# A convolution as four products side by side in the array, tokens added in place, and eight-bit tokens ahead of the FFN's transposes

## The chip, the cores and the metric

The kernel runs on one core of a Trainium2 chip. The metric is device time in microseconds of that core; lower is better. The batch of 32 images is processed in one launch.

## What is computed

The input is x, 32 images of 56 x 56 positions with 96 channels, in float32. Two layers follow each other (the weights' folding is left out here):

```python
# layer 0
h  = layernorm(x) @ w_in + b_in           # only the first 192 of 384 outputs are used
x  = x + silu(conv3x3(h, conv_w) + conv_b)  # 192 -> 96 channels, SAME padding
# layer 1, on t = x as 3136 tokens of 96 channels
a  = relu(bn1(layernorm(t) @ w1.T))       # 192 channels
X  = fft(a, axis=tokens)
X  = relu(X.re*rd - X.im*id + rb) + 1j * relu(X.im*rd + X.re*id + ib)
t  = t + bn2(ifft(X).real @ w2.T)
y  = relu(qlinear(layernorm(t), W1, b1))  # operands rounded to 8-bit floats (5, 2), sums to 16-bit
t  = t + qlinear(y, W2, b2)
```

## The kernel before

**Tiling.** An image's 3136 tokens lie as 112 partitions of 28 tokens (token = 28p + j). Partition p is half of an image row, and j is the place in that half. Work goes by groups of 4 values of j (seven groups g) or by chunks of 8, 8, 8 and 4 values (`LN_CHUNKS`).

**The convolution.** The layernorm's scaled tokens `xa` (L372) are multiplied by a constant matrix (`image`, L153), which both transposes them to channels and forms, for every four output rows, six sums of input rows; ScalarE copies them into the buffer `img` (L154). A convolution along rows then needs six products (k) of three column shifts (dx) each, instead of 4 x 3 taps x 3 shifts. `conv` (L164) does them for one chunk of j: a unit has three parts, each with two values of k and three shifts, so six matmuls of 97 rows and 96 columns of weights over 2 x n x 14 columns (224 for a chunk of 8, 112 for the chunk of 4). Part 0 is copied by ScalarE (`m`, L167), parts 1 and 2 are combined by VectorE (`sd`, L175, L176, L188, and the four output rows `s`, L183), ScalarE applies silu (L191), TensorE transposes back to tokens (`st`, L196), and VectorE adds the input (`t <- st, x`, L398). For that addition the input is loaded a second time into a buffer `x`, one DMA per chunk (L349); the first load, `xl` (L364), feeds the layernorm.

**The rest of an image.** Per group: a transpose (`tp_n`, L146), the product with w1 (`ph`, L209), relu on ScalarE (L212), the first DFT stage (`pa`, L218), a store to a DRAM scratch (`da`) and loads back in another order (`at`). Then the second stage (`px`, L233; for its third kind, u = 2, the two halves of the output are 64-column products written to partitions 0 to 63 and 64 to 127), the frequency-wise relus on both engines (`av`, `sv`, `gt`), the product with w2 and the first inverse stage (`pg`, L272 and L276, `pe`, L286), a store `de`, loads `y`, and the last stage (`py`, L294), added to `t` (L474). The FFN normalizes four tokens at a time (`xn`, float32, L488), transposes them (`tp_n`, L146), rounds them to 8 bits on ScalarE while copying them out of PSUM (`n3t`, L300), and multiplies (`pf`, L305, `po`, L322). `ffn_end` adds the result to `t` into a buffer `o` (L332), from which the output is stored (L510).

**Order.** The program is written as a plan: each step of each image has a time (`put(when, ...)`), in units of which an image takes eight, and steps are issued sorted by it. A later image starts eight units after the one before, so about four images are in flight. A scheduling pass then fixes each engine's order from these priorities and the dependencies. [...] All the DMAs of the main loop are issued by SyncE.

**Buffers.** The PSUM tag "q" (two buffers) is shared by `im`, `cv` and `st`. `pf` has one buffer. `tpool` keeps `t` of three images; `xpool` holds two of the second loads.

Two places of the plan, since their numbers matter later:

```python
for part in range(3):
    put(at + ats[part], conv_part, i, part)     # at = CONV + 2 * i, ats = (0, 0.5, 1.25)
CONV, FIRST, BACK, FFN = -12.3, -8, 8.5, 10.85
```

Of the kernel before, what the change touches and what calls it, by code (L numbers as in the profile page):

```python
# [45 lines left out]
C = 96  # L46
# [15 lines left out]
LN_CHUNKS = ((0, 8), (8, 16), (16, 24), (24, 28))  # L62


LN_W, LN_B, CONV_B, B_IN, BN1, BN2, NPAR = 0, 1, 2, 3, 5, 13, 17
# [15 lines left out]
def hybrid_kernel(ctx: ExitStack, tc: tile.TileContext, x, par, spar, w_in, conv_w, w1, w2, fw1, fb1, fw2, fb2, fa, fb, ib, ia, rows6, out):  # L81
# [7 lines left out]
    make_identity(nc, ident)  # L89
    mhalf = const.tile([N1, N2], F32, name="mhalf")  # L90
# [9 lines left out]
    convb = par_sb[:, CONV_B : CONV_B + 1]  # L100
# [40 lines left out]
    def to_channels(xs, b, g, kind):  # L141

        rows = xs.shape[2]
        ps = psum.tile([rows, G4, N1], F32, tag="tp", name=f"tp_{kind}_{b}_{g}")
        for j in range(G4):
            nc.tensor.transpose(ps[:, j, :], xs[:, j, :], ident[:N1, :N1])  # L146
        return ps

    def image(xa, n, b, j0):

        ps = psq.tile([C + 1, n, 2, WC * WG], F32, tag="q", name=f"im_{b}_{j0}")
        for j in range(n):
            nc.tensor.matmul(ps[:, j], xa[:, j, :], rows6_sb, start=True, stop=True)  # L153
        nc.scalar.copy(img[:, :, j0 + 1 : j0 + 1 + n].rearrange("c h j k g -> c j h (k g)"), ps)  # L154

    def conv(s, part, b, i):

        j0, j1 = LN_CHUNKS[i]
        n = j1 - j0
        ps = s[part] = psq.tile([C, 2, 2, n, WG], F32, tag="q", name=f"cv_{b}_{i}_{part}")  # L160
        for at, k in enumerate(PAIRS[part]):
            for dx in range(3):
                cols = img[:, :, j0 + dx : j1 + dx, k, :]
                nc.tensor.matmul(ps[:, at], wv[:, k, dx, :], cols, start=(dx == 0), stop=(dx == 2))  # L164
        if part == 0:
            m = s["m"] = work.tile([C, 2, 2, n, WG], F32, tag="m", name=f"m_{b}_{i}")
            nc.scalar.copy(m, s.pop(0))  # L167

    def conv_sums(s, b, i):

        j0, j1 = LN_CHUNKS[i]
        n = j1 - j0
        m, ps = s.pop("m"), s.pop(1)
        sd = s["sd"] = work.tile([C, 2, 2, 2, n, WG], F32, tag="sd", name=f"sd_{b}_{i}")
        nc.vector.tensor_tensor(sd[:, 0], m, ps, ALU.add)  # L175
        nc.vector.tensor_tensor(sd[:, 1], m, ps, ALU.subtract)  # L176
        s["y"] = work.tile([C, n, WG, 4, 2], F32, tag="s", name=f"s_{b}_{i}")
# [3 lines left out]
    def conv_row(s, r, at, scale):  # L181
        row = s["y"][:, :, :, r, :].rearrange("c j g h -> c h j g")
        nc.vector.scalar_tensor_tensor(row, s["sd"][:, at, 1], scale, s["sd"][:, at, 0], ALU.mult, ALU.add)  # L183

    def conv_silu(s):
# [5 lines left out]
        nc.scalar.activation(s["y"], s["y"], AF.Silu, bias=convb)  # L191

    def to_tokens(s, b, g):
        pt = psq.tile([N1, G4, C], F32, tag="q", name=f"st_{b}_{g}")
        for j in range(G4):
            nc.tensor.transpose(pt[:, j, :], s[:, j].rearrange("c r i h -> c (r i h)"), ident[:C, :C])  # L196
        return pt
# [131 lines left out]
    def ffn_add(y1, tg, o, b, g):  # L329
        y2 = work.tile([N1, G4, C], F16, tag="y2", name=f"y2_{b}_{g}")  # L330
        nc.vector.tensor_tensor(y2, y1, b2q, ALU.add)
        nc.vector.tensor_tensor(o, tg, y2, ALU.add)  # L332

    class Image:


        def __init__(self, b):
# [3 lines left out]
            self.x, self.t, self.s, self.n2t, self.hq = {}, {}, {}, {}, {}  # L341
# [3 lines left out]
        def load(self, i):  # L345
            j0, j1 = LN_CHUNKS[i]
            self.t[i] = tpool.tile([N1, j1 - j0, C + 1], F32, tag=f"t{i}", name=f"t_{self.b}_{i}")
            self.x[i] = xpool.tile([N1, j1 - j0, C], F32, tag="x", name=f"x_{self.b}_{i}")
            nc.sync.dma_start(self.x[i], self.tokens[:, j0:j1, :])  # L349

        def group(self, g, tiles=None):
            return (tiles or self.t)[g // 2][:, g % 2 * G4 : (g % 2 + 1) * G4, :]
# [21 lines left out]
    def make_image(im, i, j, n):  # L374
        image(im.xa[i][:, j : j + n], n, im.b, LN_CHUNKS[i][0] + j)

# [5 lines left out]
    def conv_part(im, i, part):  # L382
        if part == 0:
            im.s[i] = {}
        conv(im.s[i], part, im.b, i)

    def conv_first(im, i):
        conv_sums(im.s[i], im.b, i)

    def conv_last(im, i):  # L390
        conv_silu(im.s[i])

    def conv_tokens(im, g):
        im.held["st", g] = to_tokens(im.s[g // 2]["y"][:, g % 2 * G4 :], im.b, g)

    def conv_end(im, g):

        nc.vector.tensor_tensor(im.group(g)[:, :, :C], im.held.pop(("st", g)), im.group(g, im.x), ALU.add)  # L398
        for i in ended(g):
            im.rs[i] = stats(im.t[i], "b", im.b, i)  # L400

    def deviation(im, i):

        _, var, rs = im.rs[i]
        nc.vector.tensor_tensor(im.t[i][:, :, C], var, rs, ALU.mult)
# [65 lines left out]
    def back_end(im, g):  # L471
# [3 lines left out]
        for i in ended(g):  # L475
            mu, _, rs = stats(im.t[i], "c", im.b, i)
            im.norm[i] = mu, None, rs

    def normal(im, g, j):

        i = g // 2
        if j == 0:
            im.xc[g] = xnp.tile([N1, G4, C], F32, tag="xn", name=f"xn_{im.b}_{g}")
        mu, _, rs = im.norm[i]
        xc = im.xc[g]
        for j in (j, j + 1):
            at = g % 2 * G4 + j
            nc.vector.tensor_scalar(xc[:, j], im.t[i][:, at, :C], mu[:, at : at + 1], rs[:, at : at + 1], ALU.subtract, ALU.mult)  # L488
# [15 lines left out]
    def ffn_end(im, g):  # L504
        o = im.held["o", g] = work.tile([N1, G4, C], F32, tag="o", name=f"o_{im.b}_{g}")
        ffn_add(im.held.pop(("y1", g)), im.group(g)[:, :, :C], o, im.b, g)

    def store(im, g):
        o = im.held.pop(("o", g))
        nc.sync.dma_start(im.result[:, g * G4 : (g + 1) * G4, :], o)  # L510
# [8 lines left out]
    def plan(b):  # L519
# [5 lines left out]
        for i, (j0, j1) in enumerate(LN_CHUNKS):  # L525
            last = i == len(LN_CHUNKS) - 1

            at = CONV - 8 + 2 * (i + 1)
            ats = (-0.95, -0.7) if last else (0.2, 0.5, 0.85) if i == 2 else (0.25, 1.0, 1.5)
            put(at + ats[0] - (2.5 if b else 12), fetch, i)  # L530
            put(at + ats[0] - 1.15, take_in, i)
            for part, j in enumerate(range(0, j1 - j0, 3)):
                put(at + ats[part], make_image, i, j, min(3, j1 - j0 - j))

            at = CONV + 2 * i
            put(at + 0.6, im_load, i)
            ats = (0, 0.35, 0.7) if last else (0, 0.5, 1.25)
            for part in range(3):
                put(at + ats[part], conv_part, i, part)
            put(at + ats[1] + 0.2, conv_first, i)  # L540
            put(at + ats[2] + 0.2, conv_last, i)
            for g, off in zip(range(j0 // G4, j1 // G4), (1.85, 2.75)):
                put(at + off, conv_tokens, g)
                put(at + off + 0.15, conv_end, g)
            put(FIRST + 2 * i - 0.75, deviation, i)
        put(CONV - 0.6, make_seam)
        for g in range(NG):
# [7 lines left out]
            put(max(BACK - 0.6, at - 2.9), fetch_y, g)  # L555
# [27 lines left out]
    def im_load(im, i):  # L583
        im.load(i)

    CONV, FIRST, BACK, FFN = -12.3, -8, 8.5, 10.85
# [14 lines left out]
    run(CONV - 0.1)  # L601

    with tc.tile_pool(name="setup", bufs=1) as sp, tc.tile_pool(
# [4 lines left out]
        nc.sync.dma_start(spar_sb, spar)  # L608
        win = sp.tile([C, H], F32, name="win")
# [242 lines left out]
```

## Time and profile before

| | us |
|---|---|
| median of 3 runs (lowest to highest) | 3248.47 (3239.42 to 3249.1) |
| the profiled execution: its time, its span | 3247.36, 3245.6 |
| TensorE matmul busy, in the span | 3167.5 (98%) |
| TensorE weight load busy | 2737.2 (84%) |
| VectorE busy | 2529.4 (78%) |
| ScalarE busy | 2196.2 (68%) |
| GpSimd busy | 598.2 (18%) |
| granted TensorE clock, mean | 0.986 of full |
| DMA engines' mean busy share | about 0.4 |

The page is of one profiled execution. Its own time stands 1.1 us below the median, and its span is 1.8 us shorter than its time. A float32 matmul of the program appears as two records, each with its own weight load; a transpose and an eight-bit matmul appear as one. Matmuls are pipelined: a record's duration is longer than the time until the next record can start, so the starts of consecutive records tell what one costs.

### The profile page before, as it was taken

The page shows a single profiled execution, that of the slowest core. Times are in us where ns is not written, and L with a number is a line of the kernel's source. Part 1 is how long each engine was busy: PE and PEld are TensorE (multiplying, and loading weights), DVE is VectorE, ACT ScalarE, POOL GpSimd, SP SyncE. Part 2 cuts the span into 40 slices and gives each one's busy share as a digit, 9 for nine tenths or more (in the row PEclk, how much of TensorE's full clock was granted, in tenths as well). Part 3 has the DMA queues.
Part 4 walks back from the last instruction along what each step waited for, and adds up shares of the span by engine and source line. Part 5 has one row for each costly group of instructions (what it writes and reads, how often), then busy time and mean ns, then how long its engine had stood idle before and what let it go on. Part 6 is the DMA issues. An engine that isn't in the chain of part 4 may idle for free.

```text
span 3245.6 us, 66513 instructions
## 1 busy us (share of the span) xinstructions
PE 3167.5 (98%) x23701; PEld 2737.2 (84%) x23701; DVE 2529.4 (78%) x7829; ACT 2196.2 (68%) x5232; POOL 598.2 (18%) x397
## 2 busy tenths in 40 slices
PE   7999999999999999999999999999999999999997
PEld 6888888888888888888888888888888888888875
DVE  5557878877877877877877887878787878787777
ACT  2556676766776676766676766667667667767676
POOL 1211212111212111212121121111121112121111
PEclk8999999999999999999999999999999999999997
DMA  4343344343344433344333344333344333443341
GB/s 109 94 116 103 93 122 122 111 115 101 104 122 117 115 109 108 106 118 120 108 103 106 109 127 122 101 109 105 109 127 117 108 109 95 120 124 97 103 118 56
DMA packets 334551, 355.43 MB, mean 110 GB/s; under 512 B 129305, under 2 KB 287401, under 8 KB 333993
## 3 DMA queue, kind: packets, MB, share of 16 engines
q1 hardware_dynamic: 332210, 349.01, 38.6%
q8 instruction: 187, 3.06, 0.4%
q10 hardware_dynamic: 2008, 2.17, 0.2%
q14 instruction: 146, 1.19, 0.1%
HBM read 196.93 MB, written 154.14 MB: 108 GB/s over the span
## 4 chain that ended last, share of the span: by engine, by line
PE 87%; DMA 7%; DVE 3%; ACT 1%; issue 1%; SPq 0%; POOL 0%; ACTq 0%; DVEq 0%; POOLq 0%
PE cv L164 21%; PE px L233 9%; PE ph L209 9%; PE pa L218 8%; PE im L153 7%; PE tp_n L146 5%; PE pg L276 5%; PE pe L286 5%; PE pg L272 5%; PE py L294 4%; PE pf L305 4%; PE po L322 4%; DMA de<-es 2%; PE st L196 2%; DMA at<-da 2%; DMA y<-de 1%
## 5 line engine op out<-in xcount | busy, mean ns | idle before, releaser
L164 PE MATMUL cv<-img,wv 97*96 97x224 f32 (+1 forms) x4608 | 874.7, 330 | 0.2
L164 PEld LDWEIGHTS cv<-img,wv 97*96 97x96 f32 x4608 | 671.3, 164 | 101.0 <-issue 16.4
L138 POOL TENSOR_TENSOR rs_c<-var_c,mhalf 112x8 f32<-112x8 f32 (+1 forms) x128 | 198.3, 1549 | 1404.5 <-DVE var_c L136 1039.0
L307 ACT CAST h<-pf 128x448 f16<-128x448 f32 x672 | 362.2, 539 | 87.2 <-PE pf L305 86.4
L138 POOL TENSOR_TENSOR rs_b<-var_b,mhalf 112x8 f32<-112x8 f32 (+1 forms) x128 | 193.9, 1515 | 1194.7 <-DVE var_a L136 592.8
L233 PEld LDWEIGHTS px<-fb_sb,at 112*64 112x64 f32 (+1 forms) x3584 | 329.7, 165 | 94.7 <-issue 42.0
L212 ACT ACTIVATE h<-ph,rs_b 112x192 f32<-112x192 f32 x896 | 330.0, 424 | 105.7 <-PE ph L209 102.6
L233 PE MATMUL px<-fb_sb,at 112*64 112x112 f32 (+3 forms) x3584 | 378.2, 273 | 21.7 <-DMA at<-da 19.3
L209 PE MATMUL ph<-w1a,n2t 97*112 97x192 f32 x1792 | 380.2, 329 | 3.3 <-DVE sv L252 2.0
L218 PE MATMUL pa<-h,fa_sb 112*112 112x384 f32 x896 | 366.7, 491 | 0.3 <-DVE t L398 0.3
L315 DVE TENSOR_SCALAR h<-h,b1q 128x448 f16<-128x448 f16 x658 | 216.4, 329 | 178.1 <-ACT h L307 170.4
L153 PE MATMUL im<-rows_sb,xa 112*97 112x168 f32 x1792 | 333.4, 312 | 11.3 <-DVE xa L372 10.1
L209 PEld LDWEIGHTS ph<-w1a,n2t 97*112 97x112 f32 x1792 | 288.9, 177 | 32.1 <-DVE sv L252 2.6
L249 DVE SCALAR_TENSOR_TENSOR sv<-px,spar_sb,av 128x224 f32<-128x224 f32 (+2 forms) x352 | 153.9, 437 | 183.3 <-ACT av L240 180.7
L153 PEld LDWEIGHTS im<-rows_sb,xa 112*97 112x97 f32 x1792 | 262.9, 167 | 25.1 <-DVE xa L372 10.1
L219 ACT COPY u<-pa 112x384 f32<-112x384 f32 x448 | 216.2, 482 | 80.7 <-PE pa L218 76.3
L316 DVE CAST hq<-h 128x448 fp8e5<-128x448 f16 x672 | 259.2, 386 | 11.7 <-ACT h L313 6.7
L305 PE MATMUL pf<-n3t,w1q 96*128 96x448 fp8e5 x672 | 243.1, 362 | 7.4 <-ACT h L307 6.2
L276 PE MATMUL pg<-w2x,gt 128*112 128x96 f32 (+1 forms) x1792 | 245.3, 260 | 0.0
L322 PEld LDWEIGHTS <-hq 128*112 128x112 fp8e5 x2688 | 198.5, 135 | 51.7 <-DVE hq L316 16.9
L276 PEld LDWEIGHTS pg<-w2x,gt 128*112 128x112 f32 (+1 forms) x1792 | 239.8, 178 | 1.0
L488 DVE TENSOR_SCALAR xn<-t,st_c,rs_c 112x96 f32<-112x96 f32 x896 | 231.7, 324 | 10.1 <-POOL rs_c L138 7.3
(115 smaller groups left out, 6121.7 us busy)
## 6 DMA issues: line engine op xcount, KB each, us to landing
da<-u SPq DMA_DIRECT2D x224, 336.0 KB, 2.9
at<-da SPq DMA_DIRECT2D x224, 336.0 KB, 4.8
de<-es SPq DMA_DIRECT2D x448, 84.0 KB, 2.5
y<-de SPq DMA_DIRECT2D x224, 168.0 KB, 3.0
out<-o SPq DMA_DIRECT2D x224, 168.0 KB, 2.6
xl<-in_x SPq DMA_DIRECT2D x96, 336.0 KB, 3.5
x<-in_x SPq DMA_DIRECT2D x96, 336.0 KB, 4.0
xl<-in_x SPq DMA_DIRECT2D x32, 168.0 KB, 2.3
```

The lines of the kernel that those rows point to most:

```text
L138: nc.gpsimd.tensor_tensor(rs, var, mhalf[:, :n], ALU.pow)
L153: nc.tensor.matmul(ps[:, j], xa[:, j, :], rows6_sb, start=True, stop=True)
L164: nc.tensor.matmul(ps[:, at], wv[:, k, dx, :], cols, start=(dx == 0), stop=(dx == 2))
L209: nc.tensor.matmul(ph[:, j, :], n2t[:, 2 * j2 + j, :], w1a, start=True, stop=True)
L212: nc.scalar.activation(h[:, j], ph[:, j], AF.Relu, scale=rs[:, 2 * j2 + j : 2 * j2 + j + 1])
L218: nc.tensor.matmul(pa, fa_sb, h, start=True, stop=True)
L233: nc.tensor.matmul(px[rows, j], lhs, fb_sb[:, first(p) : first(p + 1)], start=True, stop=True)
L276: nc.tensor.matmul(pg[:, half, j, :], lhs, w2x, start=False, stop=True, skip_group_check=True)
L305: nc.tensor.matmul(pf, w1q[:, k * 128 : (k + 1) * 128], n3t, start=True, stop=True)
L307: nc.scalar.copy(h1, pf)
L316: nc.vector.tensor_copy(hq[:, k, :], h2, saturate=False)
L322: nc.tensor.matmul(po[:, j, :], hq[:, k, j * N1 : (j + 1) * N1], w2q[:, k, :], start=(k == 0), stop=(k == 2))
```

## The change

The unit of the convolution is now a third of the output channels over all columns, in place of all channels over a chunk of columns. A unit r has 32 output channels. The 28 columns of a half row are cut into NT = 4 stretches of CT = 7, and each stretch's product goes to its own 32 partitions of the output: four matmuls with the same 32 columns of weights and different moving data. An image has three units of three parts; a part has 2 k x 3 dx x 4 stretches = 24 matmuls of 196 columns. All but the first of a part are issued at high priority and kept in program order, so that little comes between them.

The tokens of x are put in another order beforehand (`ORDER`), so that a group of four j holds one column of each stretch; the tables `fb` and `ib` are permuted alike, and the output is put back. A token tile `t` now holds 16 or 12 values of j (`HALVES`); x is loaded straight into it (two DMAs an image instead of four into `x`), and both the convolution's result and the FFN's are added to it in place. The buffers `x` and `o` are gone, and `tpool` keeps four images. `im` goes two columns at a time. The FFN's `xn` is written as eight-bit floats, and its transpose is a plain eight-bit matmul with an eight-bit identity.

```diff
+NT, CT = 4, N2 // 4
+CB, NR = 32, 3
+HALVES = ((0, 4), (4, NG))
+ORDER = [CT * t + g for g in range(NG) for t in range(NT)]
...
-            nc.tensor.transpose(ps[:, j, :], xs[:, j, :], ident[:N1, :N1])
+            if xs.dtype == F8:
+                nc.tensor.matmul(ps[:, j, :], xs[:, j, :], ident8, start=True, stop=True)
+            else:
+                nc.tensor.transpose(ps[:, j, :], xs[:, j, :], ident[:N1, :N1])
...
-        ps = psq.tile([C + 1, n, 2, WC * WG], F32, tag="q", name=f"im_{b}_{j0}")
+        ps = psq.tile([C + 1, 2, 2, WC * WG], F32, tag="q", name=f"im_{b}_{g}_{t0}")
...
-        ps = s[part] = psq.tile([C, 2, 2, n, WG], F32, tag="q", name=f"cv_{b}_{i}_{part}")
+        ps = s[part] = psq.tile([128, 2, 2, CT, WG], F32, tag="q", name=f"cv_{b}_{r}_{part}")
         for at, k in enumerate(PAIRS[part]):
             for dx in range(3):
-                cols = img[:, :, j0 + dx : j1 + dx, k, :]
-                nc.tensor.matmul(ps[:, at], wv[:, k, dx, :], cols, start=(dx == 0), stop=(dx == 2))
+                for t in range(NT):
+                    cols = img[:, :, CT * t + dx : CT * (t + 1) + dx, k, :]
+                    w = wv[:, k, dx, r * CB : (r + 1) * CB]
+                    args = ps[t * CB : (t + 1) * CB, at], w, cols
+                    if at + dx + t == 0:
+                        nc.tensor.matmul(*args, start=True, stop=False)
+                        continue
+                    with tc.high_priority():
+                        tc.keep_in_program_order(nc.tensor.matmul(*args, start=(dx == 0), stop=(dx == 2)))
...
-        pt = psq.tile([N1, G4, C], F32, tag="q", name=f"st_{b}_{g}")
-        for j in range(G4):
-            nc.tensor.transpose(pt[:, j, :], s[:, j].rearrange("c r i h -> c (r i h)"), ident[:C, :C])
+        pt = psq.tile([N1, g1 - g0, 128], F32, tag="q", name=f"st_{b}_{r}_{half}")
+        for g in range(g0, g1):
+            nc.tensor.transpose(pt[:, g - g0, :], s[:, g].rearrange("c r i h -> c (r i h)"), ident)
...
-        nc.vector.tensor_tensor(o, tg, y2, ALU.add)
+        nc.vector.tensor_tensor(tg, tg, y2, ALU.add)
...
-            self.x[i] = xpool.tile([N1, j1 - j0, C], F32, tag="x", name=f"x_{self.b}_{i}")
-            nc.sync.dma_start(self.x[i], self.tokens[:, j0:j1, :])
+            nc.sync.dma_start(self.t[half][:, :, :C], self.tokens[:, j0 : j0 + n, :])
...
-        nc.vector.tensor_tensor(im.group(g)[:, :, :C], im.held.pop(("st", g)), im.group(g, im.x), ALU.add)
+        t = im.t[half][:, :, r * CB : (r + 1) * CB]
+        st = im.held.pop(("st", r, half)).rearrange("p j (t c) -> p (j t) c", c=CB)
+        nc.vector.tensor_tensor(t, st, t, ALU.add)
...
-            im.xc[g] = xnp.tile([N1, G4, C], F32, tag="xn", name=f"xn_{im.b}_{g}")
+            im.xc[g] = xnp.tile([N1, G4, C], F8, tag="xn", name=f"xn_{im.b}_{g}")
...
+            at = CONV - 2.45 + 0.7 * i
+            put(at - 0.55, take_in, i)
+            for j in range(0, j1 - j0, 2):
+                put(at + 0.08 * j, make_image, i, j)
+            put(CONV + 5.7 + 1.5 * i, norm_b, i)
+        put(CONV - 0.1, make_seam)
+        put(CONV, load, 0)
+        put(CONV + 1.25, load, 1)
+        for r in range(NR):
+            at = CONV + 1.85 * r
+            for part, when in enumerate((0, 0.5, 1.1)):
+                put(at + when, conv_part, r, part)
+            put(at + 0.72, conv_first, r)
+            put(at + 1.32, conv_last, r)
+            for half in range(2):
+                put(at + 1.72 + 0.23 * half, conv_tokens, r, half)
+                put(at + 1.87 + 0.23 * half, conv_end, r, half)
...
-    CONV, FIRST, BACK, FFN = -12.3, -8, 8.5, 10.85
+    CONV, FIRST, BACK, FFN = -14.95, -8.25, 8.3, 10.65
...
-    tpool = ctx.enter_context(tc.tile_pool(name="tpool", bufs=3))
-    xpool = ctx.enter_context(tc.tile_pool(name="xpool", bufs=2))
+    tpool = ctx.enter_context(tc.tile_pool(name="tpool", bufs=4))
```

In the plan of after, an image's `im` steps fill the last part of the image period ahead of it, and its nine convolution parts the first part of the next; before, chunk by chunk, both were spread over the whole period.

## The prediction

> **What bounds the kernel now.** I read the page's busy shares first, then its chain of waits, then the groups with shapes kept apart, then the chain and the timeline of one image in the middle.
>
> ```profile
> PE 3167.5 (98%) x23701; PEld 2737.2 (84%) x23701; DVE 2529.4 (78%) x7829; ACT 2196.2 (68%) x5232; POOL 598.2 (18%) x397
> PE 87%; DMA 7%; DVE 3%; ACT 1%; issue 1%; SPq 0%; POOL 0%; ACTq 0%; DVEq 0%; POOLq 0%
> ```
>
> TensorE is busy 98% and carries 87% of the chain; no engine or transfer else holds it for long. The windows by stretch say the same of the middle (98.36 us busy of the 100 from 1500 on), and leave about 53 us of idle TensorE to the first 160 and the last 150 us. The longest share of the chain, 21%, is L164, the convolution:
>
> ```profile
> L164 PE MATMUL cv<-img,wv 97*96 97x224 f32 x3456 | 743.3, 354 | 0.2
> L164 PE MATMUL cv<-img,wv 97*96 97x112 f32 x1152 | 131.4, 258 | 0.0
> ```
>
> Busy time hides what a record costs, as the ends are modelled. The chain, in order of time, shows the pace:
>
> ```profile
> 1510.61 0.90 PE im L153 x6
> 1511.51 1.15 PE cv L164 x12
> ...
> 1543.83 2.27 PE cv L164 x12
> ...
> 1549.15 0.88 PE px L233 x8
> ...
> 1554.90 0.61 PE po L322 x12
> ...
> 1557.01 0.92 PE px L233 x16
> ...
> 1561.30 0.38 PE tp_n L146 x4
> ```
>
> Twelve float32 records of 224 columns take 2.27 us, 189 ns each or 0.844 ns a column; of 112 columns, 96 ns. An eight-bit record of 96 columns takes 51 ns, a float32 transpose of 112 columns 95 ns. The two px lines matter most: eight records of 128 weight columns take 0.88 us, and sixteen of 64 weight columns, alternating between two halves of the output, 0.92 us: 57.5 ns a record against 110. Two narrow float32 products do run at once. Their price of entry is in the timeline:
>
> ```profile
> 1528.85 0.81 PE L209 MATMUL ph<-w1a,n2t 97*112 97x192 f32 x4
> 1529.59 0.77 PEld L233 LDWEIGHTS px<-fb_sb,at 112*64 112x64 f32 x16 [0.24 <-issue]
> 1529.60 0.99 PE L233 MATMUL px<-fb_sb,at 112*64 112x112 f32 x16
> 1530.51 0.30 PE L146 MATMUL tp_n<-ident,xn 112*96 112x112 f32 x1
> ```
>
> The last ph record ends by its pace (162 ns each) at 1529.50 and the transpose starts at 1530.51: 1.01 us, of which eight pairs at 112 x 0.844 = 95 ns explain 0.76. About 0.24 us go into and out of the narrow mode, and the weight loads stand idle as long.
>
> [...]
>
> **The change part by part**, per image, of which 32 run; an image's period is 98.8 us (the same pa step of the chain at 1505.41 and 1604.18).
>
> *Convolution on TensorE.* Before: 3456/32 = 108 records at 189 ns and 36 at 96 ns, 23.9 us. After: 216 matmuls, 432 records, which four at a time are 108 passes of 196 x 0.844 = 165 ns, 17.9 us. In the build order a part's 24 matmuls stand together in 273 places, twice 24 in six, 72 in one: 280 narrow blocks, 8.75 an image, at 0.24 us, 2.1 us. Net -3.9 us.
>
> *FFN transposes.* 28 an image go from 95 to about 51 ns (po's row, the nearest): -1.2 us. The transposes back, 28 of 96 columns (83 ns) before, 21 of 128 (109 ns) after, stay at 2.3 us; the 28 im matmuls stay.
>
> So TensorE loses 5.1 us an image, 163 us in all.
>
> *VectorE and ScalarE.* The sums of the convolution go from 14.9 to about 11.2 us on VectorE (nine of 392 elements at 554 ns and twelve of 196 at 516, interpolated between the rows of 448 and 224, and of 224 and 112). Adding the input: seven times 550 ns become three of 550 and three of about 680, the same. m and silu on ScalarE fall from 5.8 to 4.3 us, while im's copies rise from 11 (5.7 us) to 14 at 445 ns (6.2). [...] The in-place adds are L332's own, at no cost. These hide behind TensorE where it is fed, so I take no gain from them.
>
> *The new distribution.* The build order puts all nine blocks of an image into 42.8 us of TensorE work and none into the next 46.8 (records at their pace). In those 46.8 us I count 101 ScalarE and 146 VectorE instructions; at the rows' means they sum to 48.4 and 57.8 us. Records overlap at their ends: over the whole run the means sum to 3116 us on VectorE and 2583 on ScalarE where the page has 2529 and 2196 busy, so I scale by 0.81 and 0.85: **47 us of VectorE** and 41 of ScalarE beside 47 of TensorE. In the blocks' stretch they are 31 and 27 of 43. Before, VectorE averaged 78% with the convolution spread out. So VectorE becomes about as long as TensorE for half the period, with single buffers between (pf). Lower bound: lag is made up in the following blocks, 0. Upper: every ScalarE and VectorE hand-over of that stretch shows, 5 us. I take 2.3 us.
>
> *A longer wait.* cv's first part now needs every im copy and the seam copies of the image. In the order only 0.4 us of TensorE work (one pf and its neighbours) lies between the last im and it, while the copy (445 ns), pf's copy h (539) and a seam copy (265) stand on ScalarE: 0.4 to 1.2 us of waiting, and everything on TensorE queues behind it. It is part of the 2.3.
>
> *DMAs.* Four loads of x become two, which wait for the store of the same half four images earlier: planned 0.15 unit, 1.9 us, apart, against 2.6 us to landing, so SyncE may stand about 1 us once an image, ahead of da's and y's transfers. y's first use lies 12.1 us of TensorE work behind the last pe (7.0 before), which hides it; without that cover 1 us an image. Loads and stores break into 384-byte pieces, as de's stores do already (2.5 us to landing); queues are used 39%. DMA waits of py and px were 8.3 and 19.3 us in all: they can hardly give more. I take 0.
>
> Sum: 3245.6 - 163 + 32 x 2.3 = 3156, and 1.8 around the span: 3158; the median stood 1.1 above the profiled execution. I say **3159 us**. With the 0 to 5 us of stalls: 3085 to 3245.
>
> **Rivals.** *Cover holds:* VectorE's lag is absorbed, stalls stay as they are: 3085. For it: TensorE's idle time in the middle is under 2%; against it: the count above. *Issue-bound:* a pass is 8 instructions in 165 ns; the densest loads in the trace are 16 in 0.77 us, 48 ns a record, so a pass might take 192: +2.9 us an image, and stalls shrink behind it: 3175 to 3250. *Two at a time (slower):* the trace shows two streams, not four. If the third and fourth wait, a pass takes 330 ns and the convolution 35.7 us: +570 us, about 3700. It decides from the price of a pass: with the stalls I take, at 191 ns all is lost (2.8 us over 108 passes). Against: pairs run without loss, and nothing in the narrow block shows a third resource filling up. *VectorE sets the second half (slower):* should its waits add more than 5.1 us to the 46.8 us stretch, the gain is gone; at 7 us it is 3310. For: 47 of 47 us; against: 31 of 43 leaves time to recover. *That it does not do what it says:* the build order shows the blocks whole, so only the concurrency is open, which is the third rival.
>
> **Chances.** Forecast (3100 to 3235) 0.53, cover holds (3060 to 3100) 0.15, issue-bound 0.12, two at a time 0.08, VectorE's half 0.12. 0.3% (10 us) is about what a measurement can tell from no change. Faster: the first two and most of the third, 0.77; the same: 0.05; slower 0.18. The range from 3075 to 3270 leaves out the two-at-a-time case, half of VectorE's and the best few.
>
> **What would show it.** Right: cv records of 32 columns at about 41 ns each on the chain, 24 x 2 in 2.0 us; an idle weight load of 0.2 us ahead of each block; tp_n of xn at 50 ns; cv's chain share near 18%; TensorE idle mostly in the stretch with im, waiting for VectorE or ScalarE. Wrong: blocks of 4 us (two at a time) or 2.3 (issue); TensorE idle of over 5 us an image, with VectorE over 90% there; or a wait on t's loads or stores on SyncE that delays y or at.

## The result, and the profile after

The changed kernel took 3237.18 us in the median of ten runs (3230.49 to 3243.63), the kernel before 3244.72 beside it (ten runs, 3239.42 to 3255.07). The ratio is 0.9971 with a 95% interval of 0.996 to 0.9981: 7.5 us less, where 86 had been forecast. The profiled execution took 3234.79 us, its span 3233.0, at a granted clock (the share of full speed that TensorE was given) of 0.980 (before 0.986).

The page of the changed kernel, its busy shares and its chain of waits:

```profile
PE 3062.8 (95%) x32693; PEld 2449.3 (76%) x32693; DVE 2438.7 (75%) x7574; ACT 2155.8 (67%) x5264; POOL 676.7 (21%) x397
PE 67%; DVE 15%; DMA 8%; ACT 5%; POOL 3%; issue 2%; SPq 0%; ACTq 0%; POOLq 0%; DVEq 0%
```

TensorE fell from 98% to 95% busy and from 87% to 67% of the chain; VectorE rose there from 3% to 15%. TensorE has less to do, and more of the chain now runs through hand-overs between engines.

The work itself became cheaper as planned. In the chain of an image in the middle, the first part of the convolution, 24 matmuls or 48 records, reads:

```profile
1598.49 0.36 PE cv L178
1598.86 0.15 PE cv L178
1599.01 1.68 PE cv L182 x43
```

43 records in 1.68 us are 39 ns each, and all 48 with their start take 2.20 us; over images 8 to 30 the starts inside the full-speed blocks lie 40 ns apart. So four narrow float32 products do run at once, at the forecast price of 41 ns. To see what is lost between records, I take for each record the time to the next start less its columns at the pace (the shortest spacing that the traces show: 0.833 ns a column of a float32 record, 140 ns for im's 168 columns; half of that in eight bits, where pf's 448 columns took 188 ns at the shortest; a quarter in the narrow convolution; half in the pairs of px, 95 ns for two records of 112 columns), and sum from the pa of image 8 to that of image 30, 22 periods:

| per image, us | before | after |
|---|---|---|
| period (from pa to pa) | 97.98 | 97.66 |
| columns at the pace | 89.83 | 82.67 |
| single excesses of more than 250 ns ("gaps") | 1.01 | 4.27 |
| everything else between records | 7.15 | 10.72 |

7.16 us of work an image went, and 6.83 us of time between records came. Of these, 2.36 are the entries into the narrow blocks (8.75 at a measured 0.27), 3.26 are longer gaps, up to 0.7 a slower clock, and the remaining 0.5 or more small gaps. The beginning adds to it: the first pa starts at 88.5 us instead of 71.0. From there to the pa of image 8 the changed kernel makes up for that (722.9 us instead of 740.4), and from the pa of image 30 to the end it takes 5.4 us less.

Where are the longer gaps? The longest waits of TensorE between 700 and 3000 us (engine, line and what it waited for; total us, times, longest us), first in the kernel before, then in the changed one:

```profile
PE px L233 <- DMA at<-da: 11.7, 20, 1.7
PE py L294 <- DMA y<-de: 5.6, 11, 1.3
```

```profile
PE po L340 <- DVE hq L334: 30.1, 21, 2.3
PE cv L178 <- ACT img L403: 21.1, 23, 0.9
PE px L251 <- DMA at<-da: 17.8, 23, 2.2
```

In the changed kernel each comes about once an image; in the image shown next, all lie within about the last 10 us ahead of the convolution. The chain of waits there, in order of time:

```profile
1582.19 2.86 POOL rs_a L145
...
1585.07 0.19 DVE xa L395
1585.26 6.98 DMA xl<-in_x
1592.24 0.02 issue
1592.27 0.04 DVE st_a L139
...
1594.50 0.24 DVE h L333
1594.74 0.37 DVE gt L276
1595.11 0.31 DVE hq L334
1595.42 0.04 issue
1595.47 0.71 PE po L340 x10
```

Read it upwards: TensorE's po waited for hq, which stood on VectorE behind the statistics of the next image, and these for a load of 7.0 us that could only start when xa had freed a buffer. The windows of that period show what came together. Their columns are the window's length, the busy us and records of TensorE, its weight loads, VectorE, ScalarE and GpSimd, then the granted clock, the share of the DMA engines (over 1 where the packets' times overlap) and GB/s:

```profile
1574.00:1582.00 8.00, 8.00 (x74) 7.37 (x73) 8.00 (x33) 6.34 (x16) 6.27 (x4) 1.00 0.26 69
1582.00:1590.00 8.00, 7.35 (x64) 6.58 (x63) 6.05 (x17) 5.71 (x14) 4.64 (x3) 1.00 0.95 254
1590.00:1598.00 8.00, 6.18 (x48) 4.89 (x46) 5.51 (x18) 6.72 (x17) 0.00 (x0) 1.00 1.12 261
```

VectorE is full for 8 of 8 us until 1582; then the DMA engines are (0.95 and 1.12, against 0.13 to 0.53 in the ten windows ahead), and TensorE idles, 1.8 us in the last. The averages of 75% and 0.4 said nothing of that. It holds beyond this image: in the mean of 22 images of the middle, VectorE is busy 7.9 of the 8 us from 24 to 16 us ahead of the convolution, with TensorE at 8.0; in the two stretches of 8 us after that VectorE falls to 3.6 and 6.1, and TensorE to 7.2 and 5.7. So TensorE loses its time just after VectorE's full stretch, not in it. The kernel before has a milder form of the same end of a period (the same two windows of its trace):

```profile
1582.00:1590.00 8.00, 7.67 (x65) 6.87 (x64) 4.28 (x14) 4.55 (x10) 0.00 (x0) 1.00 0.60 159
1590.00:1598.00 8.00, 6.69 (x45) 5.33 (x44) 6.08 (x17) 4.34 (x11) 0.00 (x0) 1.00 0.65 189
```

A second cost hides behind the first. The same place four images later, in the timeline of TensorE:

```profile
1980.92 0.35 PE L323 MATMUL pf<-n3t,w1q 96*128 96x448 fp8e5 x1
1983.17 0.71 PE L340 MATMUL po<-w2q,hq 128*112 128x96 fp8e5 x10 [1.90 <-DVE hq L334]
1983.72 1.49 PE L163 MATMUL im<-rows_sb,xa 112*97 112x168 f32 x8
1985.00 0.58 PE L323 MATMUL pf<-n3t,w1q 96*128 96x448 fp8e5 x1
1986.37 0.53 PE L178 MATMUL cv<-img,wv 97*32 97x196 f32 x1 [0.78 <-ACT img L403]
...
1986.70 3.81 PE L182 MATMUL cv<-img,wv 97*32 97x196 f32 x43
```

The 43 records take 3.81 us here, 89 ns each, and the windows say why (the columns as above):

```profile
1981.40:1984.80 3.40, 1.63 (x18) 1.64 (x19) 3.18 (x12) 2.67 (x7) 0.00 (x0) 1.00 1.09 279
1984.80:1988.20 3.40, 2.62 (x27) 1.25 (x29) 2.45 (x8) 1.24 (x4) 0.00 (x0) 0.50 0.47 131
1988.20:1991.60 3.40, 3.40 (x34) 1.74 (x23) 0.00 (x0) 0.48 (x1) 0.00 (x0) 0.50 0.00 0
1991.60:1995.00 3.40, 3.40 (x29) 2.02 (x31) 1.19 (x3) 0.73 (x2) 0.00 (x0) 0.50 0.21 55
1995.00:1998.40 3.40, 3.40 (x46) 2.53 (x38) 1.82 (x4) 0.98 (x3) 0.00 (x0) 1.00 0.00 0
```

TensorE was busy 1.63 of 3.4 us, and the next three such windows ran at a granted clock of 0.50, through the first convolution block. The half-speed stretches have a pattern in these traces: all but the one that a run's end cuts off last a multiple of 3.41 us (8 of 9 in the kernel before, 15 of 16 in the changed one; this one lasts 10.24 us from 1984.78 on), and in each trace they lie on one grid of that length. Counted by the windows of that grid, over the twenty traces of this study (the first 60 and last 80 us of each apart), of 281 full-speed windows with TensorE busy under half 279 were followed by half speed, of 329 between 0.5 and 0.65 there were 88, and of 17,098 over 0.65 none; in the traces of the kernel before and the changed one alone, 10 of 10, 3 of 29 and none of 1,751. The kernel before has no half-speed stretch between 330 us and 160 us from its end, the changed one seven, 34 us long, in which at most 17 us are lost.

### The profile page after: what moved, and what is told of

Its sections match the earlier page's. It is cut to its first block, busy times and chain, and to the rows that moved or that the text cites. A ratio compares the mean times of both kernels' runs of the same rounds, so it can differ in the third digit from the quotient of the medians.

```text
span 3233.0 us, 83954 instructions
## 1 busy us (share of the span) xinstructions
PE 3062.8 (95%) x32693; PEld 2449.3 (76%) x32693; DVE 2438.7 (75%) x7574; ACT 2155.8 (67%) x5264; POOL 676.7 (21%) x397
## 4 chain that ended last, share of the span: by engine, by line
PE 67%; DVE 15%; DMA 8%; ACT 5%; POOL 3%; issue 2%; SPq 0%; ACTq 0%; POOLq 0%; DVEq 0%
PE cv L182 15%; PE px L251 7%; PE ph L227 7%; PE pa L236 7%; DMA xl<-in_x 6%; PE py L312 4%; PE cv L178 4%; PE pg L294 4%; PE pe L304 4%; PE pg L290 3%; PE im L163 3%; PE po L340 2%; PE st L214 2%; DVE xn L515 2%; PE pf L323 2%
## 5 line engine op out<-in xcount | busy, mean ns | idle before, releaser
L145 POOL TENSOR_TENSOR rs_c<-var_c,mhalf 112x8 f32<-112x8 f32 (+1 forms) x128 | 238.9, 1867 | 2347.3 <-DVE var_b L143 866.8
L182 PE MATMUL cv<-img,wv 97*32 97x196 f32 x13248 | 642.8, 334 | 0.0
L182 PEld LDWEIGHTS cv<-img,wv 97*32 97x32 f32 x13248 | 419.2, 110 | 114.9 <-issue 0.3
L251 PEld LDWEIGHTS px<-fb_sb,at 112*64 112x64 f32 (+1 forms) x3584 | 316.3, 166 | 106.8 <-DMA at<-da 44.7
L251 PE MATMUL px<-fb_sb,at 112*64 112x112 f32 (+3 forms) x3584 | 360.9, 274 | 27.3 <-DMA at<-da 26.9
L163 PE MATMUL im<-rows_sb,xa 112*97 112x168 f32 x1792 | 315.3, 316 | 11.9 <-DVE xa L395 9.7
L515 DVE TENSOR_SCALAR xn<-t,st_c,rs_c 112x96 fp8e5<-112x96 f32 x896 | 231.8, 324 | 69.3 <-POOL rs_c L145 67.1
L256 ACT ACTIVATE av<-px,spar_sb 128x224 f32<-128x224 f32 (+2 forms) x352 | 155.4, 441 | 166.3 <-PE px L251 164.4
L145 POOL TENSOR_TENSOR rs_a<-var_a,mhalf 112x8 f32<-112x8 f32 (+1 forms) x128 | 253.4, 2000 | 29.8 <-DVE var_a L143 29.8
L340 PE MATMUL po<-w2q,hq 128*112 128x96 fp8e5 x2688 | 208.8, 219 | 38.7 <-DVE hq L334 38.6
```

The costliest lines, as they stand in the source:

```text
L145: nc.gpsimd.tensor_tensor(rs, var, mhalf[:, :n], ALU.pow)
L182: tc.keep_in_program_order(nc.tensor.matmul(*args, start=(dx == 0), stop=(dx == 2)))
L251: nc.tensor.matmul(px[rows, j], lhs, fb_sb[:, first(p) : first(p + 1)], start=True, stop=True)
L340: nc.tensor.matmul(po[:, j, :], hq[:, k, j * N1 : (j + 1) * N1], w2q[:, k, :], start=(k == 0), stop=(k == 2))
L515: nc.vector.tensor_scalar(xc[:, j], im.chunk(i)[:, at, :C], mu[:, at : at + 1], rs[:, at : at + 1], ALU.subtract, ALU.mult, saturate=False)
```

## The experiments

The theories at the start: **VectorE** is full in the half of the period without convolution blocks (the prediction's step); the **late loads** of xl hold VectorE; the serial **hand-over** from the last im to cv, over ScalarE's copy and the seam (its two copies of the image's edge columns), holds TensorE. Later ones: TensorE has only **short steps** at hand there; the **crowd of transfers**; the **order** that the scheduling pass makes of every edit. "Against changed" is the difference of the two ratios to the kernel before, times 3245 us. Gaps are those over 250 ns from the pa of image 8 to that of image 30, "half speed" what it can cost at most between 330 us and 160 us from the end (half of its length); both are from the one profiled execution, which lay up to 13 us off its kernel's median (e3's above, e12's below).

| kernel | ratio to before (95%) | against changed, us | gaps, us an image | half speed, us |
|---|---|---|---|---|
| before | | | 1.01 | 0 |
| changed | 0.9971 (0.9960 to 0.9981) | | 4.27 | 17 |
| e1 | 1.0030 (1.0021 to 1.0040) | | 1.80 | 7 |
| f2 | 1.0143 (1.0127 to 1.0159) | | 1.72 | 14 |
| e2 | 1.0288 (1.0267 to 1.0310) | +103 | 6.40 | 51 |
| e3 | 0.9916 (0.9892 to 0.9940) | -18 | 4.56 | 38 |
| e4 | 1.0030 (1.0014 to 1.0046) | +19 | 3.99 | 41 |
| e6 | 0.9339 (0.9323 to 0.9355) | -205 | 2.98 | 17 |
| e7 | 1.0828 (1.0810 to 1.0846) | +278 | 4.02 | 50 |
| e9 | 0.9965 (0.9949 to 0.9981) | -2 | 1.71 | 0 |
| e10 | 1.0334 (1.0317 to 1.0351) | +118 | 5.86 | 85 |
| e12 | 1.0215 (1.0186 to 1.0245) | +79 | 7.40 | 102 |
| e13 | 1.0107 (1.0085 to 1.0129) | +44 | 5.16 | 41 |
| e14 | 1.0048 (1.0034 to 1.0062) | +25 | 4.47 | 31 |
| f1 | 0.9960 (0.9944 to 0.9976) | -4 | 3.96 | 21 |
| f3 | 0.9916 (0.9903 to 0.9929) | -18 | 3.85 | 3 |
| f4 | 0.9972 (0.9961 to 0.9983) | 0 | 4.11 | 32 |
| f5 | 1.0028 (1.0015 to 1.0042) | +18 | 3.84 | 34 |
| f7 | 0.9968 (0.9956 to 0.9981) | -1 | 3.97 | 26 |
| f8 | 1.0298 (1.0283 to 1.0313) | +106 | 5.90 | 68 |

### The two parts of the change on TensorE

**e1**, the eight-bit transposes alone, on the kernel before:

```diff
-            im.xc[g] = xnp.tile([N1, G4, C], F32, tag="xn", name=f"xn_{im.b}_{g}")
+            im.xc[g] = xnp.tile([N1, G4, C], F8, tag="xn", name=f"xn_{im.b}_{g}")
```

> The kernel before with one part of the change alone: the FFN's tokens are written as eight-bit floats and transposed by an eight-bit product. 28 transposes an image go from about 95 to about 50 ns. In the kernel before TensorE is busy 98% and no other engine holds it, so the theory that the change's loss comes from the plan around the convolution (VectorE full in the half of the period without convolution blocks) expects the full 1.25 us an image here: about -40 us against the kernel before, between -30 and -45. The rival, that a shorter TensorE step is worth little in any version because VectorE and ScalarE are close behind it everywhere, expects less than -15 us.

3255.84 us: 0.3% slower. Columns at the pace fell by 1.31 us an image as they should, and 1.9 us came between records: gaps from 1.01 to 1.80 us, and narrow px blocks from 4.1 to 5.9 per 100 us. Neither expectation foresaw a loss.

**e2**, the same part undone in the changed kernel (the opposite diff).

> The changed kernel with the FFN's tokens and their transposes back in float32: TensorE gets 28 x 45 ns = 1.25 us an image more, all of it in or near the half of the period that has no convolution blocks. If TensorE set the end there, +40 us. If VectorE sets it (main theory), or if late loads of the layernorm's input do, the added TensorE time lies beside the waiting: 0 to +12 us.

3340.14 us, +103: more than twice what TensorE's added 1.28 us an image explain. The gaps grew by 2.1 us an image, and half-speed windows followed in 19 places instead of seven. So the work added at these places was not hidden beside a wait, against what the theory of a VectorE bound expected (in e9, below, work added in the gaps was), and one edit was worth -103 in one kernel and +10 in the other.

**e6**, one of three shifts left out:

```diff
-            for dx in range(3):
+            for dx in (0, 2):
```

> The changed kernel with the middle one of the three column shifts of every convolution left out, so 72 of 216 matmuls an image are gone: at the measured 165 ns for a pass of four, 36 passes or 5.9 us an image of TensorE time, all of it inside the convolution's blocks; VectorE's and ScalarE's work is the same. If TensorE sets the pace of the blocks' stretch and the waits of the other stretch stay as they are: -5.9 us an image, -190 us. If VectorE's and ScalarE's load sets the whole period by now (lag is made up in the blocks, and a shorter block makes up less): well under half of it, -20 to -90 us.

3030.47 us: -205, the whole of the 190 and somewhat more. TensorE's time in the blocks counts in full, and VectorE, now with 7 us less of period, keeps up. **VectorE does not bound the period as a whole.** Whether its load makes the waits of the stretch without blocks is for e3 and f1.

**e7**, the blocks not held together:

```diff
-                    with tc.high_priority():
-                        tc.keep_in_program_order(nc.tensor.matmul(*args, start=(dx == 0), stop=(dx == 2)))
+                    nc.tensor.matmul(*args, start=(dx == 0), stop=(dx == 2))
```

> The changed kernel without the priority and the fixed order inside the convolution's parts. By the build order the narrow products then stand in 796 blocks instead of 280, which is 516 entries more. If an entry costs the 0.24 us that the px pairs showed, and nothing is won by the freer order: +124 us. If the freer order fills the waits at the end of the image's period (2.8 us an image, 90 us): about +35 us. If an entry costs nothing [...]: -20 to 0 us.

3515.49 us: +278. Record by record, a whole block of one part costs 0.10 us ahead of it and 0.22 behind it, 0.27 in all with what its inside saves; the torn blocks, whose records often don't come by fours, cost 0.37 in the mean. That is 24.9 x 0.37 against 8.75 x 0.27, 6.8 us an image or 220 us; the clock takes at most 32 more, and the gaps stay (4.0 us). The rest of the 278 is not accounted for. The entry's price was near, and without "nothing between" the change would have been a loss.

### What makes the gaps

**e3**, most statistics of the second layernorm left out:

```diff
-        for j in range(0, n, 2):
+        for j in range(0, 2 if kind == "b" else n, 2):
```

> The changed kernel with most of the second layernorm's statistics left out: of each chunk only the first bn_stats of the pairs is computed and its variance is used for all the chunk's tokens, so 10 of 14 bn_stats an image are gone, about 2.7 to 2.9 us of VectorE an image in the half of the period without convolution blocks; TensorE's work is the same. If VectorE's load in that half sets the period (main theory): -1 to -2.7 us an image, -30 to -85 us. If the late loads of the layernorm's input or the hand-over from the last copy of img to the convolution set it: 0 to -10 us.

3217.2 us: -18, between the theories. po's waits for hq and cv's for img are gone from the list; px now waits 42.2 us for at instead of 17.8, and pf 23.3 for h. The gaps stay, at 4.6 us. So less work on VectorE helped somewhat, but it did not take the gaps away.

**e4**, **f5**, earlier loads with a fourth buffer, by one unit and by half a unit:

```diff
-        tag, bufs = ("xn", 2) if im.b == 0 and i == 3 else ("xl", 3)
+        tag, bufs = ("xl", 4)
-            put(at - (2.8 if b else 12), fetch, i)
+            put(at - (3.8 if b else 12), fetch, i)
```

> The changed kernel with a fourth buffer for the layernorm's input (xl) and its loads issued one unit of the plan (about 12 us) earlier. In the changed kernel VectorE's statistics a wait for these loads 113 us in all, 58 more than before. If these waits are what reaches TensorE at the period's end: about -1.3 us an image, -40 us, and the waits of the statistics for the loads below 60 us. If VectorE's own load sets the end (main theory), the saved waiting is taken up by the steps that it had put off: 0 to -15 us.

> The changed kernel with a fourth buffer for xl and its loads half a unit (6 us) earlier, and two relu steps as in the changed kernel. If late loads of xl are a cause by themselves, about what they gave on top of the relu step: -10 to -25 us against the changed kernel. If the gain came from the order that both edits gave together: -5 to +30 us, as for the earlier run with loads a whole unit earlier (+17).

3254.32 and 3258.41 us: +19 and +18. The statistics' waits for xl did fall (84.5 to 48.7 us between 700 and 3000), and py now waits 33.8 us for y, up to 4.8 at once (both from e4). By the names in the traces, the order of the two is the same on every engine and for SyncE's transfers, so f5 repeats e4 and does not test another time of the loads; that the two agree within 5 us shows how well an order's price repeats. The late loads alone are not the cause, or the new order costs what they gave.

**e10**, the image sums 0.45 unit earlier (`at = CONV - 2.9 + 0.7 * i`).

> The changed kernel with the image sums (take_in, im, and the loads ahead of them) planned 0.45 unit (5.5 us) earlier, so that img and its seam are copied before the convolution's first part is due. If the serial hand-over from the last im through ScalarE and the seam to the convolution causes the loss: the waits of cv for img (21 us in the middle of the run, 0.9 us an image) go, and with them the clock's half-speed windows there: -30 to -50 us against the changed kernel. If VectorE's load in the stretch sets the end: the same work is done in a shorter stretch, the waits appear at another step, -10 to +20 us.

3355.55 us: +118. cv waits for img no more; tp_n waits 50.9 us for t and ph 21.4 for sv instead. That fits a hand-over which is only the place where the lateness shows; but this edit, too, gave a new order.

**e12**, po and the addition behind it 0.2 unit later; **e13**, **e14**, the FFN 0.3 and 0.6 unit later, and the second load of t 0.45 with it:

```diff
-            put(at + 1.0, ffn_second, g)
+            put(at + 1.2, ffn_second, g)
```

```diff
-    CONV, FIRST, BACK, FFN = -14.95, -8.25, 8.3, 10.65
+    CONV, FIRST, BACK, FFN = -14.95, -8.25, 8.3, 11.25
```

> The changed kernel with only the FFN's second product and its addition planned 0.2 unit later. In the build order the po of group 5 then stands behind the convolution's first two parts instead of ahead of the last im; the last im and pf stand directly ahead of the convolution. If the waits at the end of an image are a matter of what TensorE has at hand there (theory of the last steps: only short steps, each waiting for a copy): the wait of po for hq (1.3 us an image) goes, but cv's wait for img stays or grows, since less lies between the last im and it: 0 to -30 us against the changed kernel. If VectorE's load sets the stretch, the wait only changes its name: -5 to +10 us.

> The changed kernel with the whole FFN planned 0.3 unit (3.7 us) later against the rest, and the second load of t 0.45 unit later since its buffer comes free later. The build order then has py, two ph, px and pa of the next image among the im steps, and 8 narrow px, pa and py between the last im and the convolution's first part. Theory of the last steps: the waits before the convolution (4.3 us an image in all gaps over 250 ns) fall by half or more and the half-speed windows go: -40 to -90 us against the changed kernel. If VectorE's load of the stretch sets the period: the total of the waits stays, 0 to +15 us.

> As the kernel with the FFN 0.3 unit later, but 0.6 unit (7.4 us) later. The build order puts py, ph, px and pa of the next image among the im steps and ph, pf and 8 px between the last im and the convolution. Theory of the last steps: as before or better, -40 to -100 us against the changed kernel, less about 7 us for a later end of the last image. If VectorE's load of the stretch sets the period: +5 to +20 us from the later end alone.

3316.13, 3282.03 and 3264.36 us: +79, +44, +25, where the theory of the short steps expected gains and VectorE's at most +20. Both missed, and the theory of the short steps has nothing left that speaks for it: the build orders were as wanted, and new waits of about the same size stood elsewhere (im for img 46.0 us in e12, px for t 46.4 in e13, py for y 25.9 in e14).

**f1**, relu and rounding as one VectorE step, and **f2**, the same on the kernel before:

```diff
-            nc.vector.tensor_scalar(h2, h1, b1q[:, k : k + 1], 0.0, ALU.add, ALU.max)
-        nc.vector.tensor_copy(hq[:, k, :], h2, saturate=False)
+            nc.vector.tensor_scalar(hq[:, k, :], h1, b1q[:, k : k + 1], 0.0, ALU.add, ALU.max, saturate=False)
```

> The changed kernel with the FFN's relu and its rounding to eight bits as one VectorE instruction in place of two (h2 is no longer written in 16 bits in between): 21 instructions of 0.33 us an image are gone from VectorE, 6.8 us, about half of them in the stretch without convolution blocks. If VectorE's load in that stretch makes the waits ahead of the convolution: they fall by about half with the clock's half-speed windows, -50 to -130 us against the changed kernel. If the plan's chain of short steps does: the chain pf, h, hq, po is shorter by one step, which may give 0 to -25 us. If the late loads do: 0 to -10 us.

> The kernel before with the same one step less on VectorE, as a control. TensorE is busy 98% there and VectorE's waits reach it for about 1 us an image in all: 0 to -15 us. A gain of the size of the changed kernel's own would say that VectorE bounds both kernels alike.

f1 took 3234.23 us, -4: no difference that can be told. VectorE lost 115 us of busy time, and TensorE's waits between 700 and 3000 us in f1 read:

```profile
PE px L251 <- DMA at<-da: 40.1, 23, 3.0
PE pf L323 <- ACT h L325: 17.7, 23, 0.8
PE po L341 <- DVE hq L333: 13.3, 15, 1.5
```

po's waits halved, at's doubled. So VectorE's load alone, the prediction's cause, is not supported. It is not excluded either: VectorE stays nearly full ahead of the gaps (7.6 of the 8 us from 24 to 16 us ahead of the convolution, 7.9 in the changed kernel), and the edit also gave a new order, whose price f2 shows. f2 took 3293.77 us: **1.4% slower with less work**. Its columns at the pace are the same to 0.01 us; gaps, entries (5.9 narrow px blocks per 100 us instead of 4.1), the clock and small gaps took 1.7 us an image. The order of TensorE's work differs between the two traces, and the blocks that were torn show it; no other cause was found.

**f3**, f1 with f5's loads, then **f4**, with the inverse stage and the FFN 0.2 unit later (`BACK, FFN = 8.5, 10.85`).

> The changed kernel with one relu step, and with a fourth buffer for xl and its loads half a unit (6 us) earlier. By the build order py, ph, px and pa then stand between the im steps and the convolution. If the late xl loads hold VectorE and through it TensorE: another -20 to -60 us below the kernel with one relu step alone. If VectorE's load did it: within 15 us of that kernel.

> The kernel with one relu step and four loads, with the inverse stage (y, py) and the FFN planned 0.2 unit (2.5 us) later and the second load of t with them. If py's waits for y in it (26.6 us in the middle, 1.2 us an image) are lateness that 2.5 us of plan can cover: -20 to -40 us against that kernel. If the order that the edit gives makes waits elsewhere, as the other shifts of the plan did: 0 to +50 us.

f3 took **3218.66 us, 0.9916 of the kernel before**, the fastest of the versions that compute all of it (with one rounding to 16 bits less): two edits of -4 and +18 gave -18 together. It has two half-speed stretches in the middle instead of seven. f4 gave that back (3238.52).

**f8** and **f7**, the 672 KB load of t made to follow the convolution's first part, in the changed kernel and in f3:

```diff
+            if after is not None:
+                nc.gpsimd.tensor_copy(self.t[half][:, 0, 0:1], after[:N1, 0, 0, 0, 0:1])
```

> The changed kernel with the 672 KB load of t of each image made to follow the convolution's first part: GpSimd writes one element of it from m, which the load then overwrites. It leaves the end of the period, where the DMA engines are busy about 1.0, and comes into the convolution's stretch, where they are busy 0.1 to 0.5; xl, at, y and de then have about 2.5 us of transfer less to share with (672 KB at the 270 GB/s of the crowded window). By the build order py, ph, px and pa of the next image also move ahead of the convolution. If the crowd of transfers keeps the waits: xl lands in 5 us or less instead of 7.0, and -20 to -80 us against the changed kernel. If the order on the engines decides whatever the transfers do: 0 to +60 us, as for the other edits of the plan.

> The kernel with one relu step and four loads, with the same later load of t. If the crowd of transfers keeps the waits: py's waits for y (1.2 us an image) fall by half or more, -15 to -40 us below that kernel (about 3180 to 3205). If the order decides: 0 to +50 us.

3342.63 us (+106) and 3237.39 (17 above f3 by the ratios). In f8 xl landed in 4.7 us instead of 7.0, as wanted, and py waited 51.8 us for y, pf 38.2 for h. Thinning the crowd did what it was to do for the loads, and the time rose all the same.

### The clock

**e9**, filler into the two gaps:

```diff
+        for _ in range(3 if r + part == 0 else 0):
+            nc.tensor.matmul(ps[:C, 0].rearrange("c h j g -> c (h j g)")[:, :H], wv[:, 0, 0, :], w1a, start=True, stop=True)
...
+        for _ in range(12 if g == 5 else 0):
+            nc.tensor.matmul(po, w1q[:, :N1], w1q, start=True, stop=True)
```

> The changed kernel with filler on TensorE, whose results are overwritten: twelve eight-bit products (about 2 us) ahead of the FFN's second product of group 5 and three float32 products (about 1 us) ahead of the convolution's first part, the two places where TensorE waits at the end of an image. The build order also moves a py and two ph ahead of the convolution's first part. In all runs so far a half-speed clock follows only where TensorE was busy for under about 0.6 of a window of 3.4 us. If the idle time is what halves the clock: no such windows in the middle of the run (7 in the changed kernel, 17 us lost) and the time 0 to 20 us below the changed kernel although 3 us an image of work is added. If the clock has another cause: the windows stay and the time rises by what of the filler does not lie in waits, 0 to +60 us.

3232.14 us, within the noise of the changed kernel, with 2.9 us an image or 92 us of TensorE work added. The timeline of e9 ahead of a convolution:

```profile
1591.12 2.12 PE L341 MATMUL po<-w1q 96*112 96x384 fp8e5 x12
...
1596.95 1.20 PE L172 MATMUL cv<-w1a,wv 97*96 97x192 f32 x6
1597.98 0.82 PE L314 MATMUL py<-y,ia_sb 113*112 113x384 f32 x2
1598.63 0.82 PE L229 MATMUL ph<-w1a,n2t 97*112 97x192 f32 x4
1599.38 0.35 PE L180 MATMUL cv<-img,wv 97*32 97x196 f32 x1
```

No wait is left in these lines, and there is no half-speed window in the middle of e9. So most of the gaps are true slack of TensorE, in which it waits for something else, and the half-speed stretches of the middle (seven in the changed kernel, 34 us) went when its idle time was filled. (py and two ph also moved ahead of cv, so not all of it is the filler's.) Over the table, the half-speed column follows the times: subtract each kernel's excess over the changed one's 17 us, and e4, e9, e12, e14, f1, f3, f4, f5 and f7 all come within 16 us of the changed kernel, though they lie up to 79 from it as measured. e2, e10, e13 and f8 keep 20 to 70 us, and e3 falls to -39. That is an estimate, as the column is the most that the half speed can cost, and it is read from one execution. A second measure has the order fixed: executions of one kernel differ in their clock (0.976 to 0.981 in the ten of the changed kernel). Each set against the mean of its own kernel, the 141 executions of the 19 kernels other than the one before take 0.73 us more for each us that the clock takes (the time times what the granted clock lacks to 1), with a correlation of 0.80. So a good part of the price of a bad order is paid through the clock.

## Why the prediction was wrong, point by point

- **The convolution on TensorE: right.** 40 ns a record, 17.64 us of columns an image at the pace (forecast 17.9). The block count held; an entry costs 0.27 us, not 0.24, 0.3 us an image. The rivals of two at a time and of issue are out.
- **FFN transposes: right in size, -1.3 us** (49 ns each, forecast 51), but e1 and e2 show that the term can't be added by itself: it was worth +10 us in one kernel and -103 in the other.
- **The stalls of the new distribution: the step that failed.** The sum had 2.3 us an image, chosen between bounds of 0 and 5. Measured are 3.3 us more of gaps, up to 0.7 of clock and the rest small gaps, 4.5 together: twice the term, though inside its bounds. That is 2.2 us an image, 70 us over 32, of the 78 us between forecast and result.
- **Its cause is not borne out.** VectorE is full for a while where it was counted to be (8.00 of 8 us), but TensorE is fed there and loses its time afterwards, and without 3.6 us of VectorE's work an image (f1) the time stays. The time is close to that of the rival in which VectorE sets the second half; its sign, over 5 us of idle TensorE with VectorE over 90% there, was not seen (gaps of 4.3 us, with VectorE at 3.6 and 6.1 of 8). What VectorE's full stretch adds by freeing xl's buffers late stays open.
- **A wait of cv for img of 0.4 to 1.2 us: right**, 0.9 us an image. Taking it away (e10, e9) gained nothing.
- **DMAs at 0: too low.** "Queues used 39%" averaged over a period in which the last 16 us are full. VectorE's wait for xl went from 55 to 113 us over the run, px's for at in the middle from 11.7 to 17.8. That the crowd is the bound is not shown (f8).
- **The clock: not in the sum at all.** In the changed kernel seven half-speed stretches of the middle, 34 us, cost at most 17 us; the kernel before had none there.
- **The start: not in the sum.** 17.4 us more until the first pa. In the chain, three units of the convolution and the load of t stand ahead of the first statistics, where before a chunk of columns sufficed. This is read from the chain and was not tried; the first eight images then win it back.

**What stays open:** why this order keeps some 4 us of gaps an image, and which order wouldn't. The waits move to whatever is latest (VectorE, ScalarE, three kinds of loads) when one is relieved, and every edit of the plan was also a new order on all engines. A run with the order held fixed and one duration changed would tell the parts from the order; it wasn't tried.

## What to carry to other kernels

Where a scheduling pass fixes the orders, a part's value is not its engine time: two edits that took work off TensorE (e1) and off VectorE (f2) made the kernel before 0.3% and 1.4% slower. So look at the gaps after each edit, and reckon with the price of a new order: here the edits of the changed kernel that left TensorE's work as it was came between 0.6% faster and 3.6% slower, e7 apart. Look at the busy shares and the DMA share by stretch of a period, not over the run. Stalls that bunch cost a second time here, through the clock: by the table at most 17 us in the changed kernel and 102 in e12. So spread or fill TensorE's idle time: in these traces no window of 3.41 us with TensorE busy over 0.65 (17,098 of them) was followed by half speed.

## What the runs showed of the hardware

- Four float32 products with 32 columns of weights each ran side by side at the full pace of one: 40 ns a record of 196 columns, a quarter of 196 x 0.833 = 163. Entering cost 0.10 us and leaving 0.22, 0.27 for a whole block of 48 records with what its inside saves.
- Half clock followed 279 of the 281 full-speed windows of 3.41 us with TensorE busy under 0.5, 88 of the 329 between 0.5 and 0.65, and none of the 17,098 over 0.65. The window ahead of the half-speed stretch at 1984.78 in the changed kernel was not idle: TensorE was busy 1.63 of 3.4 us, its gap there was 1.90 us long, and three windows at half speed followed.
